# Second attention of a decoupled cross-attention kernel: four row tiles at once on packed copies of its values

## The chip, the cores and the metric

The kernel runs on one core of a Trainium2 chip. The metric is device microseconds from start to end of one execution; lower is better. Shortened below: PE is TensorE, DVE is VectorE, ACT is ScalarE, POOL is GpSimd, SP is SyncE (it issues most DMAs). PSUM is the memory that PE writes its products to, in banks of 512 fp32 values for each of 128 partitions; SBUF holds everything else on the core, HBM lies outside.

## What is computed

```python
# x (2, 2048, 640), ctx (2, 128, 384), 8 heads of 80, 4 tokens
enc, ca = ctx[:, :124], ctx[:, 124:]
hs = mha(x @ Wq, enc @ Wk, enc @ Wv)                  # text attention: 2048 queries, 124 keys
ca_q1 = einsum('btc,th->bch', ca, Wq_ca)              # 384 channels as queries
ca_q1 = ca_q1[:, np.linspace(0, 383, 2048).astype(int), :]
ca_hs1 = mha(ca_q1, x, x)                             # first attention, over 2048 rows of x
ca_hs2 = mha(ca_hs1 @ Wq, ca @ Wk_ca, ca @ Wv_ca)     # second attention, over 4 tokens
out = (hs + ca_hs2) @ Wout + b_out + x
```

All in fp32. Of the second attention only 384 rows per batch are distinct, since the queries repeat channels.

## The kernel before

The kernel computes the 384 distinct rows of the second attention for each of the two batches. Its values are multiplied with Wout beforehand (`values_weights`): a row for each pair of a head and a token, 640 columns wide, in `w2_sb`. The pairs lie in four groups, one for two heads each, that start at partitions 0, 32, 64 and 96; within a group stand 16 rows, for two batches, two heads and four tokens. So 112 rows are in use, the rows between groups are zero, and row 112 (`N2`) is `b_out`, loaded by a DMA of its own. What the second attention gives, times Wout and with the bias, is `o2`: 384 x 640 in HBM for each batch.

`second(b)` makes it. After the softmax over four tokens (`less`, an exponential on ACT, `share`), the weights lie in `p2`, 128 channels x 3 channel tiles x 8 heads x 4 tokens. `share` divides them and spreads them by two multiplications into `p2pad`, which POOL has cleared and whose column 112 it has set to one, in the places of batch b. `turn` transposes each 128 x 113 of it into a PSUM bank, ACT copies the three transposes to `p2T`, and for each of the three channel tiles and the two halves of 320 columns `by_columns` runs four matmuls of 113 x 32 against `w2_sb`, one for each 32 output partitions: four column strips, which PE runs side by side. Each product takes one of four single banks (`banks`), ACT copies it out, and when both halves of a channel tile are there, SP stores it.

An output row tile is 128 rows of x. For each, an indirect DMA on POOL (`add_second`, profile line L2324) gathers the rows of `o2` by the channel that each row uses and adds them to a buffer that was loaded with x; the tiles are called `x_more` and, for the later ones, `last_rows`. Then PE multiplies the text attention's heads (`hs`, `wout_sums`) with Wout into `po`, and DVE adds that to the buffer, which SP stores.

The first attention of a batch (`adapter`) runs in two passes over x, held in a compressed form `zop`. Pass one forms scores `s1` by four row tiles at once, each 32 rows deep and 512 columns wide, into four banks that form a single buffer, `quad` (tag `sq`); DVE takes the maximum (`mx`), and only then does the next round start. Pass two forms `s2` in the same buffer, ACT takes the exponential (`ea`), and PE contracts it with `y_sb` into `acc`. Beside this run the query projections (`pq`), the text scores (`sc`), their softmax (`m`, `p`, `r`), its transposition by DVE and DMAs (`eb`, `kept`, `pT`) and the text output (`ph`, `hs`, `po`). x comes in through `xi`, which DVE transposes to `xt`.

Every operation is a `Do(engine, function, after, needs, frees, marks, mode)`, yielded by a generator for each part of the work. `needs` names a room (a pool of buffers: `banks`, `quad`, `eas` for SBUF tiles), `frees` gives it back, `mode` is the tile shape of PE (rows, columns). The order is not found at build time: the table `TURNS` holds, for every operation, its place in one order of the whole program, so that each engine's instructions follow that order. Waits are then put in by the framework where an instruction uses what another engine or a DMA writes.

Most instructions are recorded by helpers, so a line of the profile tells the helper: L395 is `matmul`, L404 `by_columns`, L409 `transpose`, L426 any call of DVE, ACT or POOL, L446 `dma`. The trace cuts names at their numbers: it shows `po2` and `po` both as `po`, with `w_sb` for `w2_sb` among its inputs, `s1` and `s2` as `s`, `pt_p2` as `pt_p`, and `o2` as `o`.

Of the kernel before, what the change touches and what calls it, by code (L numbers as in the profile page):

```python
# [14 lines left out]
P = 128  # L15
# [50 lines left out]
class Desk:  # L66
# [19 lines left out]
        ".1": [731], ".2": [38, 53, 54, 72, 84, 96, 102, 114, 126, 144, 156, 168, 198, 216, 498, 702], ".3": [698],  # L86
        ".4": [5, 46, 64, 70, 82, 94, 112, 136, 244, 250, 262, 268, 274, 286], ".5": [414, 445, 504, 523, 594, 613,
        620], ".6": [11, 17, 138, 162, 192, 204, 330, 336, 348, 383], ".6.1": [122], ".6.2": [188], ".6.3": [302],
        ".6.4": [326], ".6.5": [152], ".6.6": [181], ".6.7": [211], ".6.8": [229], ".6.9": [343], ".6.10": [361],
        ".6.11": [368], ".7": [374, 456, 482, 824], ".8": [23, 29, 35, 174, 222, 234, 252, 276, 294, 306, 354, 426,  # L90
        474, 510, 546, 600, 636, 750, 1020, 1031], ".8.1": [320], ".8.2": [313], ".8.3": [572], ".8.4": [667],
        ".8.5": [1067, 1069, 1208, 1213, 1226], ".8.5.1": [1288], ".8.5.2": [1318], ".8.5.3": [1385], ".8.5.4":
        [1391, 1396, 1499, 1501, 1511, 1525], ".8.5.5": [1354], ".8.5.6": [1360], ".8.5.7": [1409], ".8.5.8": [1547,
        1582, 1715, 1753, 1901, 1993], ".9": [290, 389, 420, 462, 473, 540, 582, 593, 630, 648, 659, 678, 708, 720,
        774], ".9.1": [433], ".9.2": [535], ".9.3": [554], ".9.4": [608], ".9.5": [643], ".9.6": [674], ".9.7":
        [715], ".9.8": [734], ".9.9": [757], ".9.10": [794], ".10": [629, 660, 686, 764, 900, 920, 930, 991, 998,
        1008, 1046, 1050, 1076], ".11": [746, 786, 810, 828, 852, 912, 947, 953, 955, 968, 976, 1084, 1174, 1276,
        1378, 1453], ".11.1": [848], ".11.2": [836], ".11.3": [866], ".11.4": [908], ".11.5": [938], ".12": [1091,
        1095, 1280], ".13": [772, 784, 1186], ".14": [694, 1176, 1244, 1290, 1334, 1398, 1417, 1422, 1447], ".15":
        [580, 963, 984, 1056, 1248, 1260, 1343], ".15.1": [1016], ".15.2": [1118], ".15.3": [1268], ".15.4": [1303],  # L100
        ".16": [1467], ".17": [401, 1104, 1147, 1153, 1163, 1166, 1189, 1196, 1220, 1231, 1298], ".17.1": [1562,
        1576, 1604, 1654, 1745, 1751, 1942, 2638, 3298, 3574], ".18": [395, 1145], ".19": [1037, 2699], ".20": [406,
        412, 442, 454, 490, 496, 520, 532, 562, 569, 800, 806, 818, 842, 860], ".21": [875, 1788, 1825, 1831, 1841,
        1844, 1867, 1880, 1904, 1933, 2036], ".21.1": [1892, 1912, 1946, 2236, 2339, 2345, 2350, 2554, 2722, 4594],
        ".22": [887, 2147], ".23": [2123, 3653], ".24": [881, 1128, 1200, 1308, 1362, 1440, 1518, 1536, 1608, 1686,
        1716, 1818, 1884, 1914, 1986, 2106, 2117], ".24.1": [1429], ".24.2": [1555], ".24.3": [1873], ".24.4":
        [1951], ".24.5": [2159, 2161, 2216, 2225, 2227, 2300], ".24.5.1": [2248], ".24.5.2": [2254], ".24.5.3":
        [2375], ".24.5.4": [2381, 2386, 2501, 2605, 2705, 2803], ".24.5.5": [2308], ".24.5.6": [2398], ".24.5.7":
        [2513], ".24.5.8": [2837, 3022, 3185, 3271, 3281, 3361], ".25": [892, 898, 928, 982, 1102, 1114, 1126, 1138,
        1324, 1331, 1460, 1472, 1514, 1532, 1592], ".26": [1619, 2352, 2449, 2461, 2471, 2522, 2569, 2612, 2684,  # L110
        2749, 2792], ".26.1": [2504, 2566, 2624, 2776, 2957, 2963, 3016, 3316, 5062, 5350], ".27": [1631, 2927],
        ".28": [3065, 4643], ".29": [1625, 1637, 2081, 2442, 2490, 2544, 3059], ".29.1": [1851], ".29.2": [2133],
        ".29.3": [2169], ".29.4": [2187], ".29.5": [2849], ".29.6": [2921], ".29.7": [2070, 2208, 2280, 2532],
        ".29.7.1": [2754, 2874], ".29.7.1.1": [3038], ".29.7.2": [2136, 2256], ".29.7.2.1": [2293], ".29.7.3":
        [2574, 2706, 2808], ".29.7.3.1": [2660], ".29.7.3.2": [2858], ".29.7.4": [2179], ".29.7.5": [2263],
        ".29.7.6": [2366], ".29.7.7": [2557], ".29.8": [2591, 2593, 2642, 2651, 2653, 2678], ".29.8.1": [2998],
        ".29.8.2": [2668], ".29.8.3": [3101], ".29.8.4": [3389, 3400, 3551, 3637, 3659, 3661], ".29.8.5": [3250],
        ".29.8.6": [3376], ".29.8.7": [3515], ".29.8.8": [3707, 3826, 3947, 4213, 4223, 4315], ".30": [1642, 1666,
        1708, 1732, 1774, 1786, 1960, 1984, 2014, 2153, 2192, 2276, 2318, 2330, 2402], ".31": [2417, 3090, 3163,
        3169, 3179, 3206, 3289, 3434, 3464, 3517, 3632], ".31.1": [3554, 3748, 3902, 3928, 3995, 4001, 4072, 4630,  # L120
# [2444 lines left out]
```

## Time and profile before

| | us |
|---|---|
| median of 3 runs (lowest, highest) | 577.65 (577.57, 577.72) |
| profiled execution | 578.33 |
| its span, first to last instruction | 576.5 |
| PE busy | 566.8 (98%) |
| DVE busy | 395.6 (69%) |
| ACT busy | 297.4 (52%) |
| POOL busy | 151.3 (26%) |

The granted clock of PE was 1.00. 1.83 us of the profiled execution lie around the span. A page of the profile lists the instructions by line, engine, operation, output and inputs with their sum and mean; the trace behind it answers for one stretch, one engine or one tile. An engine's idle time is given with the engine or transfer that it waited for. PE's instructions come as weight loads (PEld) and matmuls; a matmul of fp32 operands leaves two records, one of the rounded type fp32r leaves one. Several matmuls in different strips or row tiles run side by side, so the sum of their durations says little; the start of the next group says how long they held PE.

### The profile page before, as it was taken

What the parts mean: (1) busy time and instruction counts of PE and PEld (TensorE: products, weight loads), DVE (VectorE), ACT (ScalarE), POOL (GpSimd) and SP (SyncE); (2) the same over time, 40 slices, a digit from 0 to 9 for tenths busy, and PEclk for the clock granted to TensorE, in tenths of its full rate; (3) what the DMA queues carried; (4) which work ended last, traced back from release to release, by engine and by line L of the source; (5) the groups of instructions that cost most, each with busy time, mean ns of one, the idle gap of its engine ahead of it and who ended that gap; (6) DMA issues with size and microseconds to landing.
All of it is one profiled execution on the core that took longest, in us unless ns stands there. A gap on an engine that the chain in (4) does not pass through costs nothing.

```text
span 576.5 us, 18994 instructions
## 1 busy us (share of the span) xinstructions
PE 566.8 (98%) x8115; PEld 311.3 (54%) x8115; DVE 395.6 (69%) x666; ACT 297.4 (52%) x840; POOL 151.3 (26%) x211
## 2 busy tenths in 40 slices
PE   9999999999999999999999999999999999999997
PEld 8885335455556455465554554554454454445463
DVE  2465899999998567468899999998243224435363
ACT  1222355565668698999957572634564763100000
POOL 8202023041520005301014151313332211345151
PEclk9999999999999999999999999999999999999999
DMA  7998475878748785535574988865676556879988
GB/s 221 225 247 128 145 152 154 180 181 177 208 117 177 219 231 137 177 111 182 181 238 145 321 273 241 239 231 157 164 208 192 147 155 213 222 191 260 280 164 226
DMA packets 145214, 112.70 MB, mean 195 GB/s; under 512 B 82405, under 2 KB 116581, under 8 KB 145130
## 3 DMA queue, kind: packets, MB, share of 16 engines
q1 hardware_dynamic: 139210, 100.47, 60.7%
q0 software_dynamic: 5632, 10.69, 11.0%
q8 instruction: 64, 1.05, 0.7%
q10 hardware_dynamic: 288, 0.33, 0.2%
q14 instruction: 20, 0.16, 0.1%
HBM read 71.23 MB, written 40.22 MB: 193 GB/s over the span
## 4 chain that ended last, share of the span: by engine, by line
PE 73%; DVE 13%; DMA 5%; ACT 4%; issue 3%; POOL 0%; SPq 0%; DVEq 0%; ACTq 0%
PE po L404 24%; PE pq L404 13%; PE acc L395 7%; PE ph L395 6%; PE s L395 6%; DVE mx L426 5%; PE sc L395 5%; PE pq L395 4%; PE pyz L395 2%; ACT ea L426 2%; ACT p L426 2%; DVE eb L426 2%; DMA x_more<-in_x_dram 1%; PE pv L395 1%; PE pk L395 1%
## 5 line engine op out<-in xcount | busy, mean ns | idle before, releaser
L426 DVE TENSOR_REDUCE mx<-s 128x4 f32<-128x2048 f32 x48 | 109.0, 2270 | 2.8 <-PE s L395 2.7
L426 ACT ACTIVATE p<-sc,m 128x124 f32<-128x124 f32 x256 | 90.2, 375 | 37.4 <-DVE m L426 37.4
L426 ACT ACTIVATE ea<-s 128x2048 f32<-128x2048 f32 x48 | 90.6, 1887 | 36.3 <-PE s L395 36.3
L404 PE MATMUL po<-wout_sums,hs 128*32 128x320 f32 x1024 | 78.6, 433 | 1.5 <-DVE x_more L426 1.5
L404 PE MATMUL po<-wout_sb,hs 128*32 128x320 f32 x928 | 72.0, 434 | 0.0
L404 PE MATMUL pq<-xt,wq_sb 128*32 128x256 f32 (+1 forms) x928 | 65.9, 418 | 0.0
L426 DVE TENSOR_TENSOR last_rows<-last_rows,po 128x320 f32<-128x320 f32 x60 | 28.2, 481 | 49.3 <-PE po L404 48.8
L426 DVE TENSOR_TENSOR x_more<-x_more,po 128x320 f32<-128x320 f32 x68 | 32.4, 481 | 42.4 <-PE po L404 40.7
L426 ACT ACTIVATION_READ_ACCUMULATOR p<-sc,m 128x1 f32 x256 | 55.4, 216 | 0.0
L404 PEld LDWEIGHTS po<-wout_sums,hs 128*32 128x32 f32 x1024 | 33.0, 110 | 34.4 <-DVE x_more L426 2.0
L426 POOL TENSOR_TENSOR p<-p,r 128x992 f32<-128x992 f32 x11 | 20.4, 1852 | 117.1 <-DVE r L426 117.1
L395 PE MATMUL acc<-ea,y_sb 128*32 128x384 f32 (+2 forms) x768 | 50.3, 383 | 0.2 <-ACT ea L426 0.2
L395 PE MATMUL ph<-pT,vpad 128*32 128x256 f32 x768 | 48.1, 381 | 0.1
L2324 POOL DMA_INDIRECT x_more<-o,query x17 | 26.7, 1568 | 80.6 <-DVE x_more L426 47.7
L426 DVE TENSOR_REDUCE m<-sc 128x4 f32<-128x496 f32 x64 | 40.8, 659 | 8.7 <-PE sc L395 8.6
L404 PEld LDWEIGHTS po<-wout_sb,hs 128*32 128x32 f32 x928 | 29.5, 110 | 30.1 <-issue 1.6
L404 PEld LDWEIGHTS pq<-xt,wq_sb 128*32 128x32 f32 x928 | 28.2, 110 | 28.3 <-issue 13.6
L426 DVE STREAM_TRANSPOSE eb<-p 128x1024 f32<-128x1024 f32 x32 | 39.4, 1232 | 2.7 <-ACT p L426 1.6
L395 PEld LDWEIGHTS sc<-kmain,q 64*128 64x128 f32 x512 | 31.2, 187 | 14.6 <-issue 7.4
L426 POOL TENSOR_TENSOR hs<-hs 128x256 f32<-128x256 f32 x32 | 25.7, 833 | 50.7 <-ACT hs L426 30.2
L395 PE MATMUL sc<-kmain,q 64*128 64x124 f32 x512 | 37.2, 284 | 0.0
L426 POOL TENSOR_TENSOR x_sums<-xt,x_sums 128x512 f32<-128x512 f32 x10 | 13.7, 1365 | 84.8 <-DVE x_sums L426 84.5
(219 smaller groups left out, 857.4 us busy)
## 6 DMA issues: line engine op xcount, KB each, us to landing
kept<-eb SPq DMA_DIRECT2D x32, 512.0 KB, 3.7
pT<-kept SPq DMA_DIRECT2D x16, 1024.0 KB, 8.1
landing<-away SPq DMA_DIRECT2D x15, 512.0 KB, 4.4
xi<-in_x_dram SPq DMA_DIRECT2D x56, 128.0 KB, 4.3
x_more<-in_x_dram SPq DMA_DIRECT2D x17, 320.0 KB, 5.2
out_dram<-x_more SPq DMA_DIRECT2D x16, 320.0 KB, 4.1
last_rows<-in_x_dram SPq DMA_DIRECT2D x15, 320.0 KB, 4.9
out_dram<-last_rows SPq DMA_DIRECT2D x14, 320.0 KB, 4.0
```

Source lines behind the costliest of these rows:

```text
L395: self.pin(self.nc.tensor.matmul(out, lhsT, rhs, **kw))
L404: self.pin(self.nc.tensor.matmul(out[j : j + 32], lhsT[:, j : j + 32], rhs, **kw))
L426: self.pin(getattr(engine, what)(*args, **kw))
L2324: desk.pin(nc.gpsimd.indirect_dma_start(out=t, out_offset=None, in_=o2_of[b], in_offset=bass.IndirectOffsetOnAxis(ap=query[:, st : st + 1] ...
```

## The change

The values are brought into a form in which 32 rows suffice for a batch: eight heads by four tokens, without the rows of the other batch and without zeros. `w2_sb` becomes 128 x 2 x 320. The products of `values_weights` are first put there as before, in 112 rows; half of `b_out`, broadcast to 16 rows by its DMA, is added to the first 16 rows, which are the first group, two heads, for both batches. Since each head's weights sum to one, the two halves make the whole bias. Four DMAs store the groups to HBM as `rows_w2`, 32 rows for each batch, and two for each batch bring them back: the left and the right half of the columns, 32 partitions each, twice.

`share` becomes one multiplication in place. `turn` turns the weights by matmuls with the identity in four column strips: it places the 32 rows of two channel tiles, each of them twice, in the four groups of partitions; a second set does so for the third channel tile. One copy brings both to `p2T`. The products then run in row tiles of 32 x 128 with 320 columns: a round of four, for two channel tiles and both halves, then one of two for the third tile. A round writes one bank of `quad` for each of its matmuls. Each channel tile is copied out by one copy of 640 columns, on ACT or on DVE, and stored. `quad` is given back after the copies of a round; the step that closes it after the last batch (`more`) now waits for it. The order of all work, the table `TURNS`, is another one; some instructions change engines with it (softmax scalings from ACT to POOL, sums of `hs` from DVE to POOL, copies).

```diff
@@ the table TURNS
-        ".1": [731], ".2": [38, 53, 54, 72, 84, 96, 102, 114, 126, 144, 156, 168, 198, 216, 498, 702], ".3": [698],
-        ".4": [5, 46, 64, 70, 82, 94, 112, 136, 244, 250, 262, 268, 274, 286], ".5": [414, 445, 504, 523, 594, 613,
...
+        ".1": [995], ".2": [38, 53, 54, 72, 84, 96, 102, 114, 138, 156, 162, 168, 204, 210, 804, 972], ".3": [590],
+        ".4": [5, 46, 64, 70, 82, 94, 112, 136, 244, 250, 262, 268, 274, 286], ".5": [420, 446, 468, 487, 534, 553,
...
@@
     krest = const.tile([P, 4, B, NK], F32R, name="krest")
     vpad = [const.tile([P, HEADS, VH + 2 * VR], F32, name=f"vpad_{b}") for b in range(B)]
     y_sb = const.tile([P, NSB, 4, 2, 4, G], F32, name="y_sb")
-    w2_sb = const.tile([N2 + 1, H], F32, name="w2_sb")
-    p2pad = const.tile([P, NCC, P], F32, name="p2pad")
+    w2_sb = const.tile([P, B, HALF], F32, name="w2_sb")
     query = const.tile([P, NST], mybir.dt.uint32, name="query")
     cap = ctx.enter_context(tc.tile_pool(name="cap", bufs=1))
     small = ctx.enter_context(tc.tile_pool(name="small", bufs=4))
@@
     for t in (caT, cadT, blk["k"], blk["v"]):
         nc.gpsimd.memset(t, 0.0)
     wqcaT = sp.tile([P, NCH, T], F32, name="wqcaT")
+    bias = sp.tile([2 * B * T, H], F32, name="bias")
@@
         def last():
             for h in range(HEADS):
                 dma(wout_sb[VR * h : VR * (h + 1), 4, :], Wout[D * h + VH : D * (h + 1), :], 0.1, 0.42, 1.6)
-            dma(w2_sb[N2:, :], b_out[None, :], 0.1)
+            dma(bias, b_out[None, :].to_broadcast([2 * B * T, H]), 0.1)
         yield Do("SP", last, marks=[("wout", 2)])
@@
                 "PE", product, ["blk v"] + [("wout", k) for k in range(3)], needs=[(banks, 1)]
             )
             yield evacuate(
-                w2_sb[:N2, cols], op.value[:N2], op.slots[0][0], after=[op.at], marks=[("w2", u)]
+                w2_sb[:N2, u, :], op.value[:N2], op.slots[0][0], after=[op.at], marks=[("w2 rows", u)]
+            )
+
+        def add_bias():
+            to = w2_sb[: 2 * B * T].rearrange("p u n -> p (u n)")
+            desk.v_scalar_tensor_tensor(to, bias, 0.5, to, ALU.mult, ALU.add)
+
+        yield Do("DVE", add_bias, [("w2 rows", 0), ("w2 rows", 1), ("wout", 2)], marks=["w2 made"])
+        rows_w2 = hbm.tile([B, G, H], F32, name="rows_w2")
+        for g in range(4):
+            yield Do(
+                "SP",
+                lambda g=g: dma(
+                    rows_w2[:, 2 * T * g : 2 * T * (g + 1), :],
+                    w2_sb[G * g : G * g + 2 * B * T].rearrange("p u n -> p (u n)"), 0.25, 0.42,
+                ),
+                ["w2 made"], marks=[("w2 out", g)],
+            )
+        for b in range(B):
+            halves_of_b = rows_w2[b].rearrange("k (u n) -> u k n", u=2)
+            yield Do(
+                "SP", lambda b=b, of=halves_of_b: [
+                    dma(w2_sb[2 * G * i : 2 * G * (i + 1), b, :], of, 0.45, 0.42) for i in range(2)
+                ],
+                [("w2 out", g) for g in range(4)], marks=[("w2", b)],
             )
     def text_values():
@@
                 desk.g_memset(e.rearrange("p h (j k) -> p h j k", j=4)[:, :, :, NK // 4 :], 0.0)
         yield Do(
-            "POOL", go, ["v done", "keys", "query", "wy 1", "wy 0", ("w2", 0), ("w2", 1), "wz"],
+            "POOL", go, ["v done", "keys", "query", "wy 1", "wy 0", "w2 made", "wz"],
             marks=["late"],
         )
@@
     def second(b):
-        def clear():
-            desk.g_memset(p2pad, 0.0)
-            desk.g_memset(p2pad[:, :, N2 : N2 + 1], 1.0)
-
-        op = yield Do("POOL", clear, [])
-        cleared = op.at
         N = NCC * HEADS
         s2 = s2f.rearrange("p a h t -> p (a h) t")
         p2 = small.tile([P, N, T], F32, tag="p2", name=f"p2_{b}", bufs=1)
@@
         def share():
             desk.v_tensor_reduce(r2, p2, AX.X, ALU.add)
             desk.v_reciprocal(r2, r2)
-            p2of = p2.rearrange("p (a g j) t -> p a g j t", a=NCC, j=2)
-            r2of = r2.rearrange("p (a g j x) -> p a g j x", a=NCC, j=2, x=1)
-            for j in range(2):
-                k0 = 2 * T * b + T * j
-                desk.v_tensor_tensor(
-                    p2pad[:, :, : 4 * G].rearrange("p a (g k) -> p a g k", g=4)[:, :, :, k0 : k0 + T],
-                    p2of[:, :, :, j, :], r2of[:, :, :, j, :].to_broadcast([P, NCC, 4, T]), ALU.mult,
-                )
-            desk.spent += 0.43
-
-        op = yield Do("DVE", share)
+            desk.v_tensor_tensor(p2, p2, r2.unsqueeze(2).to_broadcast([P, N, T]), ALU.mult)
+            desk.spent += 0.3
+
+        yield Do("DVE", share)
+        rounds = ((0, 1), (2,))
         def turn(s):
             pt = bank(s[0], f"pt_p2_{b}")
-            for ct in range(NCC):
-                transpose(pt[: N2 + 1, ct * P : (ct + 1) * P], p2pad[:, ct, : N2 + 1], ident)
+            for n, of in enumerate(rounds):
+                for g in range(4):
+                    ct = of[g // 2 % len(of)]
+                    matmul(
+                        pt[G * g : G * (g + 1), n * P : (n + 1) * P],
+                        p2[:, ct * HEADS : (ct + 1) * HEADS, :].rearrange("p h t -> p (h t)"), ident,
+                        start=True, stop=True, skip_group_check=True,
+                    )
             return pt
-        op = yield Do("PE", turn, [op.at, cleared], needs=[(banks, 1)])
+        op = yield Do("PE", turn, needs=[(banks, 1)], mode=(P, 32))
         pt, s = op.value, op.slots[0][0]
         def out_of(e):
-            t = ea_tile(e[0], f"p2T_{b}")[: N2 + 1, 0, :]
-            copy(t, pt[: N2 + 1, :CAD])
+            t = ea_tile(e[0], f"p2T_{b}", 512)[:, 0, : 2 * P]
+            copy(t, pt[:, : 2 * P])
             return t
         op = yield Do("ACT", out_of, needs=[(eas, 1)], frees=[(banks, s)])
         p2T, i = op.value, op.slots[0][0]
         here = op.at
         o2_of[b] = hbm.tile([CAD, H], F32, tag=f"o2_{b}", name=f"o2_{b}")
-        for ct in range(NCC):
-            op = yield Do("NONE", lambda e: ea_tile(e[0], f"o2_{b}_{ct}"), [here], needs=[(eas, 1)])
-            o2, k = op.value.rearrange("p g k -> p (g k)")[:, :H], op.slots[0][0]
-            for u in range(2):
-                cols = slice(u * HALF, (u + 1) * HALF)
-
-                def product(s, u=u, cols=cols):
-                    po = bank(s[0], f"po2_{b}_{ct}_{u}")
-                    by_columns(
-                        po[:, :HALF], p2T[:, ct * P : (ct + 1) * P], w2_sb[:, cols],
+        op = yield Do("NONE", lambda e: ea_tile(e[0], f"o2_{b}", 512), [here], needs=[(eas, 1)])
+        o2, k = op.value.rearrange("p g k -> p (g k)")[:, : NCC * H].rearrange("p (a n) -> p a n", a=NCC), op.slots[0][0]
+        for n, of in enumerate(rounds):
+
+            def product(s, n=n, of=of):
+                q4 = late["sq"].tile([P, 4, 512], F32, tag="sq", name=f"po2_{b}_{n}")
+                for g in range(2 * len(of)):
+                    part = slice(G * g, G * (g + 1))
+                    matmul(
+                        q4[:, g, :HALF], p2T[part, n * P : (n + 1) * P], w2_sb[part, b, :],
                         start=True, stop=True,
                     )
-                    return po
-
-                op = yield Do("PE", product, [here, ("w2", u)], needs=[(banks, 1)], mode=(P, 32))
-                op = yield Do(
-                    "ACT", lambda po=op.value, cols=cols: copy(o2[:, cols], po[:, :HALF]),
-                    frees=[(banks, op.slots[0][0])], marks=[("o2 part", b, ct, u)],
-                )
-            yield Do(
-                "SP", lambda: dma(o2_of[b][ct * P : (ct + 1) * P, :], o2, 1.2, 0.37),
-                [("o2 part", b, ct, 0), ("o2 part", b, ct, 1)], frees=[(eas, k)],
-                marks=[("o2 out", b, ct)],
-            )
-        yield Do(
-            "NONE", lambda: None, [("o2 out", b, ct) for ct in range(NCC)], frees=[(eas, i)],
-            marks=[("o2", b)],
-        )
+                return q4
+
+            op = yield Do("PE", product, [here, ("w2", b)], needs=[(quad, 1)], mode=(32, P))
+            for c, ct in enumerate(of):
+                yield Fork(one(Do(
+                    EITHER,
+                    lambda q4=op.value, c=c, ct=ct: copy(
+                        o2[:, ct].rearrange("p (u n) -> p u n", u=2), q4[:, 2 * c : 2 * c + 2, :HALF]
+                    ),
+                    [op.at], marks=[("o2 part", b, ct)],
+                )), 0)
+                yield Fork(one(Do(
+                    "SP", lambda ct=ct: dma(o2_of[b][ct * P : (ct + 1) * P, :], o2[:, ct], 1.2, 0.37),
+                    [("o2 part", b, ct)], marks=[("o2 out", b, ct)],
+                )), 0)
+            yield Do("NONE", lambda: None, [("o2 part", b, ct) for ct in of], frees=[(quad, 0)])
         if b == B - 1:
-            def more():
+            def more(at):
                 sq_stack.close()
                 late["ps"] = ctx.enter_context(tc.tile_pool(name="ps_r", bufs=1, space=bass.MemoryType.PSUM))
                 banks.at += [desk.now] * 4
-            yield Do("NONE", more, [])
+            yield Do("NONE", more, [], needs=[(quad, 1)])
+        yield Do(
+            "NONE", lambda: None, [("o2 out", b, ct) for ct in range(NCC)], frees=[(eas, i), (eas, k)],
+            marks=[("o2", b)],
+        )
     sq_stack = ExitStack()
     early_stack = ExitStack()
```

406 rows, old and new, of the table TURNS are left out of this document.

## Prediction

> **What bounds the kernel now.** I read the page's first part, then who holds TensorE up.
>
> ```profile
> PE 566.8 (98%) x8115; PEld 311.3 (54%) x8115; DVE 395.6 (69%) x666; ACT 297.4 (52%) x840; POOL 151.3 (26%) x211
> PE po L404 <- DVE x_more L426: 1.5, 2, 1.1
> PE s L395 <- ACT ea L426: 1.2, 2, 1.0
> PE s L395 <- DVE mx L426: 1.2, 2, 0.8
> ```
>
> TensorE (PE) is busy for 98% of the span, and its waits (total, times, longest) are tiny: 1.5 us for a finished output row, 2.4 us for the score buffer. So PE's own work is the first account, and a microsecond of it is a microsecond of time, unless another engine is nearly full as well. Whether one is, the table by stretch says, here its sums over the first attention of each batch, 65 to 178 us and 276 to 388 us:
>
> ```profile
> sum 113.00, PE 112.49 PEld 56.28 DVE 111.73 ACT 68.09 POOL 28.08; mean PE 18.75 PEld 9.38 DVE 18.62 ACT 11.35 POOL 4.68
> sum 112.00, PE 110.91 PEld 59.18 DVE 106.08 ACT 66.89 POOL 28.02; mean PE 22.18 PEld 11.84 DVE 21.22 ACT 13.38 POOL 5.60
> ```
>
> VectorE (DVE) is 99% busy in the first and 95% in the second, where 5.9 us are free. Both engines bind there together. Outside of these, PE alone binds (DVE is at 69% over the whole). Batch 0's second attention falls into the second stretch, batch 1's lies later, where DVE has room.
>
> **What is removed.** The order of PE for batch 0 (o2 is the second attention's output, `po2` its product, `pt_p2` the turning of its weights, `s1` the next scores), before and then after:
>
> ```order
> L409 MATMUL pt_p2_0_3959<-ident_69,p2pad_111 113x128 x3
> L404 MATMUL pq_7_0_3761<-xt_1_3_2898,wq_sb_98 32x256 x8
> L404 MATMUL pq_7_3_3978<-x_sums_841,wq_sb_98 32x256 x16
> L404 MATMUL po2_0_0_0_4000<-w2_sb_110,p2T_0_3974 32x320 x4
> L395 MATMUL s1_1_0_2_0_4008<-zop_1_0_3223,cop_153 128x512 x4
> L404 MATMUL po2_0_0_1_4018<-w2_sb_110,p2T_0_3974 32x320 x4
> ```
>
> ```order
> L395 MATMUL pt_p2_0_3942<-ident_69,p2_0_3697 32x128 x8
> L404 MATMUL pq_7_0_3750<-xt_1_3_2987,wq_sb_98 32x256 x8
> L395 MATMUL po2_0_0_3965<-w2_sb_110,p2T_0_3959 128x320 x4
> L404 MATMUL pq_7_3_3973<-x_sums_872,wq_sb_98 32x256 x16
> L395 MATMUL s1_1_0_2_0_3998<-zop_1_0_3211,cop_153 128x512 x4
> L404 MATMUL pq_7_4_4006<-xt_1_3_2987,wq4_99 32x512 x8
> ```
>
> A product of four column strips per channel tile and half becomes a round of four row tiles, for two channel tiles and both halves: two rounds a batch for six groups. The round takes the score buffer (`quad`), so it stands between two `s1` that need the same buffer. Their prices, from PE's timeline (start, length, tile, matmul records; an fp32 matmul leaves two records, a score matmul one):
>
> ```profile
> L404 PE MATMUL po<-w_sb,p2T 113*32 113x320 f32 x96 | 8.7, 435 | 0.1
> 346.72 0.72 PE L404 MATMUL po<-wout_sb,wout_sums 128*32 128x320 f32 x8
> 347.37 0.50 PE L395 MATMUL s<-zop,cop 32*128 32x512 f32 x4
> 347.81 2.90 PE L404 MATMUL po<-wout_sb,hs 128*32 128x320 f32 x40
> 350.64 0.51 PE L395 MATMUL s<-zop,cop 32*128 32x512 f32 x4
> 293.42 0.58 PE L409 MATMUL pt_p<-ident,p2pad 128*113 128x128 f32 x3
> 293.93 1.07 PE L404 MATMUL pq<-xt,wq_sb 128*32 128x256 f32 x16
> 294.82 1.91 PE L404 MATMUL pq<-x_sums,wq_sb 128*32 128x256 f32 x32
> ```
>
> Forty records (five groups of four) hold PE from 347.81 to 350.64, so 2.83; eight (one group) from 346.72 to 347.37, so 0.65. The difference of four groups is 2.18: 0.54 a group, with 0.11 for the change of shape to `s`. The 96 records are 12 groups: 6.5 us go. The old turning is 0.51 a batch (293.42 to 293.93): 1.0 goes. In all 7.5 us.
>
> **What is added on PE.** No row shows fp32 matmuls in four row tiles. The nearest are `s`, four row tiles of 512 columns in 0.44 (347.37 to 347.81), which is one pass, and fp32 in two row tiles, against fp32 alone:
>
> ```profile
> 288.76 1.16 PE L395 MATMUL sc<-kmain,q 64*128 64x124 f32 x16
> 289.68 0.64 PE L395 MATMUL sc<-krest,rests 64*128 64x124 f32 x8
> 44.90 1.78 PE L395 MATMUL pv<-w_v,ctxT 128*128 128x320 f32 x6
> 46.52 0.60 PE L409 MATMUL pt_a<-ident,a 128*128 128x128 f32 x4
> ```
>
> A whole fp32 matmul of 320 columns takes 0.54 (1.62 for three, 44.90 to 46.52), so 124 columns would take 0.21; eight of them in two row tiles took 0.92 (288.76 to 289.68) and not 1.67. So fp32 row tiles do run two at once, and four at once I take as 0.54 a round, the price of one: four rounds, 2.2. The bounds are this and 12 x 0.54 = 6.5, if all run one after the other. A round stands alone among strips, so it pays a change of shape, about 0.12: 0.5. The new turning is two groups of four strips of 128 columns a batch; strips of 256 columns took 0.89 for two groups (293.93 to 294.82), so 0.22 a group, 0.9 in all, with no change of shape around it. Added 3.5; **net on PE -4.0**.
>
> The Trainium skill (TensorE: Matmul & The Clock Gate, Measured speedup vs the span model) gives four row tiles of 512 columns as 3.07 times as fast, not 4 times. By that a round would be about 0.70 and the forecast 0.6 us later, an estimate from that page; this trace's four `s` in 0.44 speak for full overlap.
>
> **The copies out and the shared buffer.** Six copies of 320 columns a batch, all on ACT, become three of 640, on ACT or DVE.
>
> ```profile
> L426 DVE COPY hs<-ph 128x512 f32<-128x512 f32 x14 | 9.3, 683 | 7.1 <-PE ph L395 7.1
> L426 DVE COPY hs<-ph 128x256 f32<-128x256 f32 x3 | 1.2, 416 | 0.0
> L426 ACT COPY hs<-ph 128x512 f32<-128x512 f32 x18 | 10.5, 590 | 24.7 <-PE ph L395 24.6
> L426 ACT COPY o<-po 128x320 f32<-128x320 f32 x12 | 5.2, 430 | 15.1 <-PE po L404 15.1
> 508.00 0.04 issue
> 508.75 0.03 issue
> 508.77 0.02 DVEq L426
> 508.79 0.04 issue
> ```
>
> Carried on along each pair of rows, 640 columns are 0.82 on DVE and 0.70 on ACT. In the built order one engine's copy waits for the other's, so the buffer is held for both in sequence. A handover costs about 0.09 (0.03, 0.02 and 0.04 in the chain). After a round the next use of `quad` thus comes 0.82 + 0.70 + 3 x 0.09 = 1.8 us later. Batch 0's first round has 16 `pq` matmuls ahead of `s1`, 32 records, about 1.8: cover just fits, but two softmax reductions stand ahead of DVE's copy. The wait lies between 0 and 0.7; I take 0.35. Batch 1, before and then after (`po_9`, `po_12` are output rows, `ph_9` the text attention's values):
>
> ```order
> L395 MATMUL ph_9_0_6359<-pT_9_5766,vpad_1_108 32x256 x8
> L409 MATMUL pt_p2_1_6369<-ident_69,p2pad_111 113x128 x3
> L395 MATMUL ph_9_2_6375<-pT_9_5766,vpad_1_108 32x256 x8
> L404 MATMUL po2_1_0_0_6388<-w2_sb_110,p2T_1_6384 32x320 x4
> L395 MATMUL ph_9_4_6394<-pT_9_5766,vpad_1_108 32x256 x8
> L404 MATMUL po2_1_0_1_6406<-w2_sb_110,p2T_1_6384 32x320 x4
> ```
>
> ```order
> L395 MATMUL pt_p2_1_6353<-ident_69,p2_1_6237 32x128 x8
> L404 MATMUL po_9_2_6363<-wout_sb_100,hs_0_4125 32x320 x12
> L395 MATMUL po2_1_0_6383<-w2_sb_110,p2T_1_6377 128x320 x4
> L404 MATMUL po_9_0_6339<-wout_sums_4124,hs_0_4125 32x320 x8
> L395 MATMUL po2_1_1_6399<-w2_sb_110,p2T_1_6377 128x320 x2
> L404 MATMUL po_9_1_6403<-wout_sums_4124,hs_0_4125 32x320 x8
> ```
>
> Between its two rounds stand only two groups, 1.08: PE waits 1.8 - 1.1 = **0.7**, and between 0 and 1.5 with a busy ACT ahead. What is queued behind is PE's whole stream.
>
> **DVE.** In the second stretch PE now asks for the same scores in 2 us less, while DVE's work there stays the same (its instructions counted in both orders, each at its row's mean). The free 5.9 us shrink to 3.9; I charge 0.4 for tighter meetings, between 0 and 2.0 (all of batch 0's gain).
>
> **The late end.** The chain that ended last:
>
> ```profile
> 509.75 0.33 POOL x_more L2324
> 512.35 1.56 POOL last_rows L2324
> 514.22 6.45 DMA x_more<-o,query
> 520.68 5.37 DMA out_dram<-x_more
> 526.12 7.73 DMA x_more<-in_x_dram
> 533.94 0.50 DVE x_more L426
> 534.48 13.15 PE po L404 x192
> ```
>
> Batch 1's o2 reaches its first output rows at 514; they are stored, their buffer is loaded anew, and PE waits for that at 533, two waits and 1.5 us with the longest at 1.1. The new order finishes o2 some groups earlier (two rounds close together instead of six groups spread over PE's row), so the gathers start earlier. I count the longest wait as gone, **-1.1**, between -1.5 and 0.
>
> **Edits at nothing.** Scalings of the text probabilities on POOL:
>
> ```profile
> L426 POOL TENSOR_TENSOR p<-p,r 128x992 f32<-128x992 f32 x11 | 20.4, 1852 | 117.1 <-DVE r L426 117.1
> ```
>
> ACT's softmax scalings that move to GpSimd (POOL): six more at 1.85 are 11 us of the 425 that POOL has free, over the whole kernel; nothing I saw is waiting for one. The clearing of `p2pad` and one of two small multiplications: off the path. Half the bias, 16 rows of 640: one DVE instruction under 1 us in the 99% stretch, replaced by work moved out; uncovered, 1 us. The values' copies go out to HBM in four DMAs and back in four on SyncE (SP), and are needed 200 us later; only what is queued behind them matters (below).
>
> **The sum.** -4.0 + 0.35 + 0.7 + 0.4 - 1.1 = -3.65 (unrounded -3.6). The profiled execution is 578.33 us: 576.5 of span and 1.83 around it. It becomes 574.7, and the median of the runs, 0.68 below it, 574.0.
>
> **The rivals.** *PE alone counts:* no added wait and both late waits gone, -4.0 - 1.5, 572.2. For it: PE's waits are tiny now.
>
> *DVE binds the second stretch:* batch 0's 2.0 us and its 0.35 come to nothing, 0.4 is still paid; -2.0 + 0.7 + 0.4 - 1.1 = -2.0, 575.7. For it: 95% of DVE; against: 5.9 us free. The Trainium skill (TensorEngine Tiling (Array Packing), PSUM Bottleneck) warns that after a fourfold speedup of TensorE the copy out of PSUM may become the bottleneck; here that is the 1.8 us held after a 0.54 round. If the bias and a later second half of the values also delay the first stretch by 1.5, 577.2: no change.
>
> *Row tiles don't overlap:* 4.3 more on PE, 578.3: no change. Against: the `sc` rows.
>
> *SP becomes late, the other side:* SP's order near 90 to 105 us, before and then after (`xi` are loads of x that DVE transposes, `rows_w2` and `w2_sb` the values' copies out and back):
>
> ```order
> L446 DMA xi_0_3_885<-in_x_dram 32x16x32
> L446 DMA kept_1_1139<-eb_1_0_1129 512x1x256
> L446 DMA y_0_1_963<-yt_0_1_1_1017 512x1x128
> L446 DMA away_1_1107<-x_sums_841 32x4x256 x2
> L446 DMA away_1_1107<-wq_sums_821 32x4x256
> L446 DMA y_sb_109<-y_0_1_963 32x4x256
> L446 DMA landing_823<-away_1_1107 128x1x1024
> L446 DMA away_1_1107<-wq_sums_821 32x4x256
> L446 DMA xi_1_0_1238<-in_x_dram 32x32x32
> ```
>
> ```order
> L446 DMA xi_0_3_800<-in_x_dram 32x16x32
> L446 DMA rows_w2_816<-w2_sb_110 2x8x640
> L446 DMA y_sb_109<-y_0_0_669 32x4x256
> L446 DMA y_0_1_971<-yt_0_1_1_1023 512x1x128
> L446 DMA kept_1_1150<-eb_1_0_1140 512x1x256
> L446 DMA away_1_1092<-x_sums_872 32x4x256
> L446 DMA away_1_1092<-wq_sums_835 32x4x256
> L446 DMA away_1_1092<-x_sums_872 32x4x256
> L446 DMA w2_sb_110<-rows_w2_816 64x1x320 x2
> L446 DMA away_1_1092<-wq_sums_835 32x4x256
> L446 DMA w2_sb_110<-rows_w2_816 64x1x320 x2
> ```
>
> Where loads and stores of the first attention followed each other, copies stand between, and those coming back wait for those going out.
>
> ```profile
> 65.14 0.58 SPq L446 DMA_DIRECT2D first_rests<-away  x1
> 70.44 0.54 SPq L446 DMA_DIRECT2D y<-yt  x1
> o<-o SPq DMA_DIRECT2D x6, 320.0 KB, 3.0
> L426 DVE STREAM_TRANSPOSE xt<-xi 128x512 f32<-128x512 f32 x35 | 22.7, 679 | 1.6 <-DMA xi<-in_x_dram 1.6
> ```
>
> Eight issues at 0.54 are 4.3 us, and a wait for a landing 3.0: 7.3. DVE has no free time there, and has waited for `xi` already. If all of it reached DVE, -3.6 + 7.3, 581.4; slower from 4.8 us on. Against: `xi` was late in one wait of 1.6 us over the kernel, and SP issued nothing there from 65.7 to 70.4, 4.7 us that can take most of the new ones.
>
> **How the numbers follow.** Forecast 0.55 (572.6 to 575.2), PE alone 0.09, DVE binds the second stretch 0.16, both stretches 0.06, no overlap 0.04, SP late 0.10. The likeliest is 574.0. The range takes the first three, 0.80: 572.0 to 576.6. What this measurement can tell from no change is 0.2%, 1.2 us: faster below 576.5, 0.80; the two cases near 577 to 578, 0.10; slower 0.10.
>
> **What would show it.** Four `po2` rounds of about 0.55 each on PE; a wait of PE near 0.7 ahead of batch 1's second round, on DVE's copy; no wait near 533; DVE's sums in the two stretches still 111 to 112 and about 106, in 113 and 110 us. I am wrong if a round takes over 1 us, if batch 1's output still meets its rows late, or if DVE shows idle time on `xi` between 65 and 178 us.

## The result, and the profile after

The changed kernel takes 580.99 us (median of 20 runs, 579.60 to 586.82) against 577.90 for the kernel before (20 runs): 1.0062 times its time, 95% interval 1.0040 to 1.0083. Forecast was 574.0, within 572.0 to 576.6. The profiled execution took 581.29, with a span of 579.4 against 576.5. The ratios here and below leave out three runs of the experiments that came out slow (583.82 of `wide_back`, 586.64 of `late_back` and 944.77 of `before_wide`), which the medians and the counts of runs include.

Who holds TensorE up now (the page's first part, and the waits of PE: total, times, longest):

```profile
PE 565.4 (98%) x8069; PEld 308.1 (53%) x8069; DVE 398.2 (69%) x659; ACT 282.0 (49%) x793; POOL 166.0 (29%) x219
PE sc L395 <- ACT p L426: 2.2, 2, 1.4
PE ph L395 <- DMA pT<-kept: 1.6, 1, 1.6
PE s L395 <- ACT ea L426: 1.4, 3, 1.0
PE po L404 <- DVE hs L426: 1.3, 2, 0.8
PE unread L395 <- DVE zeros L426: 1.1, 1, 1.1
PE pt_x L409 <- DMA xz<-in_x_dram: 0.8, 1, 0.8
PE s L395 <- DVE mx L426: 0.8, 2, 0.4
PE po L395 <- DVE o L426: 0.5, 1, 0.5
```

The wait for `x_more` (1.5 us) is nearly gone, as forecast, and the one ahead of batch 1's second round (`po <- DVE o`, 0.5) is there. New and not forecast are the first two rows and the fourth. The largest loss lies where DVE is full. The stretch 105 to 125 us, first of the kernel before, then of the changed one (busy times of PE, PEld, DVE, ACT, POOL; clock; DMA share; GB/s):

```profile
105.00:125.00 20.00, 19.95 (x328) 11.39 (x316) 19.91 (x27) 11.12 (x46) 6.89 (x5) 1.00 0.83 181
```

```profile
105.00:125.00 20.00, 17.81 (x256) 9.65 (x248) 16.96 (x23) 10.88 (x43) 5.34 (x4) 0.91 0.76 154
```

PE stands still for 2.2 us of it, DVE for 3.0, and PE's clock falls to 0.91 in the mean. What led there is read from the changed kernel's SP issues (start, length), then ACT's timeline (first of the kernel before, where no wait stands ahead of the cast, then of the changed one), then the chain that ended last:

```profile
100.29 1.16 SPq L446 DMA_DIRECT2D w_sb<-rows_w  x2
101.55 0.56 SPq L446 DMA_DIRECT2D away<-wq_sums  x1
102.17 1.15 SPq L446 DMA_DIRECT2D w_sb<-rows_w  x2
103.83 0.56 SPq L446 DMA_DIRECT2D y<-yt  x1
104.49 1.01 SPq L446 DMA_DIRECT2D landing<-away  x1
```

```profile
108.51 0.63 ACT L426 CAST rests<-landing 128x512 fp32r<-128x512 f32 x1
```

```profile
114.02 0.62 ACT L426 CAST rests<-landing 128x512 fp32r<-128x512 f32 x1 [4.60 <-DMA landing<-away]
```

```profile
104.49 9.51 DMA landing<-away
...
115.15 2.08 ACT p L426 x12
...
118.50 1.55 PE sc L395 x22
```

`landing` is a load of 512 KB on which the text scores' second term waits; its fifteen loads in the kernel before took 3.8 to 5.6 us, this one 4.8. Here one is issued right behind the four copies back of the values and takes 9.51. ACT stands 4.6 us for it, with the text softmax (`p`) queued behind; PE's next scores (`sc`) wait for that softmax's buffer, and DVE's next maximum stands behind the softmax's reciprocal. Then PE runs at half clock:

```profile
115.00:118.00 3.00, 1.30 (x14) 0.48 (x6) 0.94 (x2) 3.00 (x17) 1.53 (x1) 1.00 0.66 195
118.00:122.00 4.00, 3.50 (x42) 2.21 (x42) 3.02 (x4) 3.41 (x15) 0.00 (x0) 0.76 0.98 168
122.00:126.00 4.00, 4.00 (x60) 1.98 (x64) 4.00 (x4) 1.89 (x11) 0.00 (x0) 0.81 1.15 153
```

4 us at 0.76 and 4 at 0.81 are 1.7 us lost, one piece of 3.41 us at half clock. So this place costs 2.2 + 1.7 = 3.9 us, as much as the change takes off PE's work:

```profile
296.97 0.64 PE L395 MATMUL pt_p<-ident,p 128*32 128x128 f32 x16
297.43 1.05 PE L404 MATMUL pq<-xt,wq_sb 128*32 128x256 f32 x16
298.46 0.82 PE L395 MATMUL po<-w_sb,p2T 32*128 32x320 f32 x8
299.21 1.93 PE L404 MATMUL pq<-x_sums,wq_sb 128*32 128x256 f32 x32
...
500.69 0.81 PE L395 MATMUL po<-w_sb,p2T 32*128 32x320 f32 x4 [0.51 <-DVE o L426]
501.43 1.00 PE L404 MATMUL po<-wout_sums,hs 128*32 128x320 f32 x10
```

A turning holds PE 0.46 (296.97 to 297.43), a round 0.75 (298.46 to 299.21) or 0.74, changes of shape included. Two turnings and four rounds are 3.9 us; in the kernel before the same slots were 7.8.

### The profile page after: what moved, and what is told of

It is laid out like the page before. It is cut to its first block, busy times and chain, and to the rows that moved or that the text cites. A ratio compares the mean times of both kernels' runs of the same rounds, so it can differ in the third digit from the quotient of the medians.

```text
span 579.4 us, 18870 instructions
## 1 busy us (share of the span) xinstructions
PE 565.4 (98%) x8069; PEld 308.1 (53%) x8069; DVE 398.2 (69%) x659; ACT 282.0 (49%) x793; POOL 166.0 (29%) x219
## 4 chain that ended last, share of the span: by engine, by line
PE 78%; DVE 9%; DMA 6%; ACT 3%; SPq 2%; issue 2%; DVEq 0%; ACTq 0%
PE po L404 26%; PE pq L404 17%; PE acc L395 7%; PE sc L395 6%; PE ph L395 6%; PE s L395 6%; PE pq L395 4%; DVE mx L426 3%; DMA landing<-away 3%; PE pyz L395 2%; DMA pT<-kept 1%; SPq L446 1%; ACT ea L426 1%; PE pk L395 1%; DMA xz<-in_x_dram 1%
## 5 line engine op out<-in xcount | busy, mean ns | idle before, releaser
L404 PE MATMUL po<-wout_sb,hs 128*32 128x320 f32 x1024 | 79.1, 434 | 0.9 <-DVE hs L426 0.8
L426 POOL TENSOR_TENSOR p<-p,r 128x992 f32<-128x992 f32 x17 | 32.4, 1906 | 146.5 <-DVE r L426 146.5
L404 PE MATMUL pq<-xt,wq_sb 128*32 128x256 f32 (+1 forms) x928 | 67.2, 424 | 0.0
L426 POOL TENSOR_TENSOR hs<-hs 128x256 f32<-128x256 f32 x37 | 34.7, 992 | 58.5 <-DVE hs L426 40.1
L404 PEld LDWEIGHTS po<-wout_sb,hs 128*32 128x32 f32 x1024 | 32.6, 110 | 33.3 <-issue 1.7
L395 PE MATMUL ph<-pT,vpad 128*32 128x256 f32 x768 | 46.6, 380 | 1.6 <-DMA pT<-kept 1.6
L2346 POOL DMA_INDIRECT last_rows<-o,query x15 | 23.3, 1551 | 55.0 <-DVE last_rows L426 41.5
```

Of the source, the lines that this page charges most:

```text
L395: self.pin(self.nc.tensor.matmul(out, lhsT, rhs, **kw))
L404: self.pin(self.nc.tensor.matmul(out[j : j + 32], lhsT[:, j : j + 32], rhs, **kw))
L426: self.pin(getattr(engine, what)(*args, **kw))
L2346: desk.pin(nc.gpsimd.indirect_dma_start(out=t, out_offset=None, in_=o2_of[b], in_offset=bass.IndirectOffsetOnAxis(ap=query[:, st : st + 1] ...
```

## The experiments

My theory after the traces: the four copies back are cut so that few of the DMA engines carry them. Counted in the trace's packet records, their 256 packets of 1280 bytes lie between 101.6 and 110.8 us at 55 ns each (median), which is 14 us of packet time in 9.2: one or two engines of sixteen at a time. If so, a load that is spread over all engines waits behind them on those. The rivals: eight more DMAs on SP make `landing` late, however they are cut; or the new order puts ACT's cast where it would wait anyway.

**The copies cut in another way** (`wide_back`), and **moved away** (`late_back`):

```diff
-            halves_of_b = rows_w2[b].rearrange("k (u n) -> u k n", u=2)
...
-                    dma(w2_sb[2 * G * i : 2 * G * (i + 1), b, :], of, 0.45, 0.42) for i in range(2)
...
+                    dma(
+                        w2_sb[G * q : G * (q + 1), :, :],
+                        rows_w2[:, :, HALF * (q % 2) : HALF * (q % 2 + 1)].rearrange("b k n -> k b n"), 0.45, 0.42,
+                    )
+                    for q in (2 * b, 2 * b + 1)
```

> The changed kernel, its four copies back from HBM cut in another way: each brings 32 partitions of both batches (rows of 1280 bytes, 64 of them, outermost dimension 32) instead of 64 partitions of one batch (outermost dimension 2). Same bytes, number, place in SP's order. Theory (few DMA engines: the copies as written run 128 packets one after another on two of the 16 DMA engines, and the load 'landing' behind them takes 9.5 us instead of 4.4, ACT stands 4.6 us, PE 2.2 us, and the clock then halves for 3.4 us): landing within 5.5 us, ACT's wait for it under 1 us near 110, no clock drop, 3 to 4 us less than the changed kernel: 577.2, about the kernel before. Rival (number: eight more DMAs on SP issue landing 3.4 us late): nothing changes, 581. Rival (order: in the new order ACT's cast stands ahead of the softmax and would wait anyway): 581.

Measured: 576.86 (13 runs), 0.9985 times the kernel before (0.9968 to 1.0003), where the changed kernel has 1.0062: 4.1 us less by the medians. DVE and PE are full again from 105 to 125 us:

```profile
sum 20.00, PE 20.00 PEld 11.42 DVE 20.00 ACT 12.78 POOL 5.33; mean PE 20.00 PEld 11.42 DVE 20.00 ACT 12.78 POOL 5.33
```

Both rivals had said 581. The order of all work and the number of DMAs are those of the changed kernel. `landing` is issued at 103.56 us here, and ACT hardly waits for it:

```profile
108.92 0.62 ACT L426 CAST rests<-landing 128x512 fp32r<-128x512 f32 x1 [0.28 <-DMA landing<-away]
```

So it took 5.3 us, within the 5.5 that were forecast. The same 256 packets of the copies lie within 2.8 us now (100.7 to 103.5 us, by the packet records). The execution that was profiled is the longest of the 13, 583.82; its pieces at half clock lie near 431 to 437 and 557 us, none of them here.

`late_back` keeps the narrow cut and changes two numbers of the order's table:

```diff
-        1636, 1648, 1834, 2020, 2398, 2440], ".15": [682, ...
+        1636, 1648, 1834, 2020, 5482, 5488], ".15": [682, ...
```

> The changed kernel with the same four narrow copies back, moved in SP's order by about 110 us, into the second pass of the first attention (near 215 us), where DVE is not full. Few DMA engines: landing takes 4 to 5 us and is issued 2 us earlier, no wait of ACT near 110, 577.2; a transfer near 215 us takes longer, at no cost. Number of DMAs: the four stores stay, the four loads go, so about half is won: 579. Order: 581.

Measured: 579.80 (12 runs), 1.0013 (0.9991 to 1.0036), less was won than the 577.2 of my theory; by its time alone this can't be told from "about half is won". The trace tells them apart: `landing` takes 5.2 us (issued at 104.05, ACT's cast at 109.27 behind a wait of 0.27), so the loss near 110 us is gone. It has come up at another place. The narrow copies are issued at 207.4 us there, and the next store behind them, `kept` (512 KB, median 3.7 us in the kernel before), takes twice its time; the chain of this kernel runs through it to the softmax, for which PE waits 1.1 us at 221, a wait that no other kernel here has there:

```profile
210.90 7.88 DMA kept<-eb
```

Half of its runs have a piece at half clock (a mean clock of 0.997 or less). Moving narrow copies moves their cost.

**The same loads in the kernel before**, ahead of the same `landing`, cut narrow (shown) and wide (`x[b, : 2 * G, :n]` as the source):

```diff
+    filler = const.tile([P, 256], F32, name="filler")
...
+        def land():
+            if m == 2:
+                for b, (to, n) in enumerate(((p2pad.rearrange("p a k -> p (a k)"), 320), (filler, 256))):
+                    for i in range(2):
+                        dma(to[2 * G * i : 2 * G * (i + 1), :n], x[b, :G, : 2 * n].rearrange("k (u n) -> u k n", u=2), 0.45, 0.42)
+            dma(t.rearrange("p g n -> p (g n)"), by_rows, 2.0, 0.56)
```

> The kernel before with four loads of x added right ahead of that landing, as the copies back are cut: 64 partitions each, outermost dimension 2, rows of 1280 bytes twice and of 1024 bytes twice (there is no room for more); nothing reads them. Few DMA engines: landing takes 8 to 10 us; it has 3 us of room in this order, so ACT's cast comes 4 us late, the softmax 1.5 to 2 us, and the time rises by 1.5 to 3.5 us: 579.2 to 581. Number: landing is issued 2.4 us later, within its room, and takes 4.4: 577.7, at most 578.2. Order: 577.7.

> The same four extra loads ahead of landing in the kernel before, with the same bytes, rows and partitions, but read from 64 rows of x, so that the outermost dimension is 64. Few DMA engines: landing takes 4 to 5.5 us, the time is the kernel before's within 0.6: 577.7 to 578.3. Number: the same as with the narrow loads.

Measured: narrow 582.87 (6 runs), 1.0087 (1.0067 to 1.0107), wide 578.95, 1.0017 (1.0002 to 1.0032). By the ratios, four small loads cost 5.0 us or 1.0 us, by their cut alone. Both times lie above what I had expected (579.2 to 581, and 577.7 to 578.3). The landings in the first attention of batch 0 (shortest, median, longest), narrow and then wide, and the stretch 105 to 125 us of the narrow one:

```profile
DMA to landing us min/median/max: 4.5/5.1/9.0
```

```profile
DMA to landing us min/median/max: 3.9/4.7/6.0
```

```profile
sum 20.00, PE 17.60 PEld 10.78 DVE 16.28 ACT 9.05 POOL 6.88; mean PE 17.60 PEld 10.78 DVE 16.28 ACT 9.05 POOL 6.88
```

The narrow kernel has the changed kernel's loss in the old order: a landing of 9.0 us, PE still for 1.97 us at 115 us, then 3.41 us at half clock. Of the 5.0 us, 1.7 are the clock's, which I had left out. The number of DMAs counts as well, by about a fifth of it. The Trainium skill (DMA: Bandwidth & Descriptors, Rules for kernel authors) says that an outermost dimension of size c below 16 confines a DMA to at most c engines; for c = 2 these traces agree, with one or two engines at a time in the changed kernel and 9.0 us against 6.0 here. Which engines carried a packet is not shown by the profile, so the count rests on the packet times.

**The clock.** Is it PE's own idle time that halves it?

```diff
-                        for g in range(4):
+                        for g in 5 * (0, 1, 2, 3) if (b, sb, ct, u) == (0, 2, 0, 0) else range(4):
```

(`hold_more` has 8 for 5.)

> The changed kernel, with one score round (batch 0, third block of x, first channel tile) computed five times over, on PE alone: 1.8 us more of PE's work right where it stands still near 116 us waiting for the softmax. The copies and the late landing stay. Theory: PE's clock halves for 3.4 us after PE stood still for 2.2 us out of 2.7; with under 1 us left of that the clock stays at 1.00 and 1.7 us are won though PE does more: 579.3. Rival (the halving has another cause, or the stall is DVE's and ACT's alone): 581, or up to 582.5 with PE's extra work.

> The changed kernel with the same score round computed eight times over (3.1 us more of PE's work), so that PE has hardly any idle time near 116 us; the copies, the late landing and ACT's wait stay. With five times the clock had still halved, after a gap of 1.4 us that lay in one stretch of 3.41 us between two possible changes of the clock. Theory (PE's idle share in one such stretch halves the clock in the next): no stretch at half clock near 120 us; 1.7 us are won there and up to 0.5 lost to the extra work, so about 579.3 and the stretch 118 to 122 at a clock of 1.00. Rival (the halving belongs to the stall of the whole chain, not to PE's idle time): a clock of 0.5 for 3.4 us as before.

With five times (579.57, 10 runs; 1.0041, 1.0016 to 1.0066) the clock still halved in the profiled execution: the second wait stayed whole. So the time that I had named came out, but not for the reason that I gave. With eight times the wait is 0.56 and the clock stays. PE's timeline and the stretch after it, first of `hold_clock`, then of `hold_more`:

```profile
118.27 0.94 PE L395 MATMUL sc<-kmain,q 64*128 64x124 f32 x12 [1.41 <-ACT p L426]
```

```profile
118.00:122.00 4.00, 3.73 (x42) 2.35 (x42) 3.08 (x4) 3.41 (x15) 0.00 (x0) 0.70 1.07 173
```

```profile
118.12 0.94 PE L395 MATMUL sc<-kmain,q 64*128 64x124 f32 x12 [0.56 <-ACT p L426]
```

```profile
118.00:122.00 4.00, 3.88 (x62) 2.64 (x66) 3.90 (x5) 3.41 (x14) 0.00 (x0) 1.00 1.04 176
```

ACT's wait was the same (4.7 and 4.5 us), so the idle time of PE decides. The mean clocks of all runs agree, though they don't say where a halved piece lies: one below 0.998 is in 16 of the changed kernel's 20 runs, in 5 of 10 with five times and in 2 of 12 with eight times. The time of this second kernel, 580.33 (12 runs; 1.0034, 1.0012 to 1.0056), missed the 579.3 that I had named: its extra scores delay DVE, and in its profile PE waits 1.0 us for DVE near 131 us instead.

**What a round costs** (each round computed nine times, on top of `wide_back`):

```diff
-                for g in range(2 * len(of)):
+                for g in [g for _ in range(9) for g in range(2 * len(of))]:
```

> The kernel wide_back with each of the four row-tile rounds computed nine times over, to read what a round costs on PE without the changes of tile shape around it: full overlap 0.54 each, and 32 more are 17 us; as the Trainium skill's 3.07 for four tiles would have it about 0.70, 22 us; one after the other 2.2 for a round of four. A round of two matmuls costs the same 0.54 with full overlap.

```profile
293.41 5.13 PE L395 MATMUL po<-w_sb,p2T 32*128 32x320 f32 x72
298.47 0.42 PE L404 MATMUL pq<-x_sums,wq_sb 128*32 128x256 f32 x4
```

Measured: 593.58 (one run), 16.7 us above `wide_back`'s median. Nine rounds hold PE 5.06, one held it 0.75: 4.31 for eight, 0.54 each; a round of two gives the same (5.04). So four fp32 row tiles overlap fully. The Trainium skill (TensorE: Matmul & The Clock Gate, Measured speedup vs the span model) gives 3.07 for four row tiles, by which a round would be about 0.70, an estimate; these rounds don't bear it out. The change of shape around a round is 0.75 - 0.54 = 0.21.

**The wait that the new order brings.** In the changed kernel PE waits 1.6 us near 433 us for `pT`, a load of 1 MB (in the profile of `wide_back` 2.9, of `late_back` 1.2). The chain of the changed kernel shows the load issued when the text output before it had given its buffer back, and 8.66 us on the way:

```profile
425.48 0.86 PE ph L395 x16
426.34 0.06 PE po L404
426.40 8.66 DMA pT<-kept
435.06 0.04 issue
435.11 1.05 PE ph L395 x13
```

Between lie 7.1 us of PE's work. The table of the order was edited so that 2.4 us more lie between, in `wide_ph` with the three products next to each other, in `wide_ph2` apart:

```diff
-        ".71.3": [10817, 10871, 10876, 11010, 11034, 11124, 11135], ".71.3.1": [11053], ".71.3.2": [11102],
+        ".71.3": [10817, 10871, 10876, 11118, 11130, 11148, 11159], ".71.3.1": [11119], ".71.3.2": [11132],
```

```diff
-        ".71.3": [10817, 10871, 10876, 11010, 11034, 11124, 11135], ".71.3.1": [11053], ".71.3.2": [11102],
+        ".71.3": [10817, 10871, 10876, 11082, 11118, 11166, 11177], ".71.3.1": [11089], ".71.3.2": [11120],
```

> The kernel wide_back with three products of one text output (unit 15, ph) moved on PE behind two output rows, two contractions and a score round, 2.4 us of work: in the new order PE reaches ph 1.2 to 2.9 us before its 1 MB load pT has landed (8.7 us after its buffer came free); the kernel before had no such wait. If that wait is a loss of its own, from the new order and not from the copies, it goes: 1.2 to 2.5 us less than wide_back, 575; with it goes a halved clock in some runs. If it only moves to the next use of the load, or the moved work then waits itself: 576.9 as wide_back.

> The kernel wide_back with the three products of unit 15's text output moved back by 2.4 us of PE's work as in wide_ph, but kept apart by contractions and score rounds, so that their copies out keep up. In wide_ph the wait for the load pT went and two waits for those copies came, 1.6 us. If that was all, PE has no wait over 0.5 us near 430 and the kernel gains 1.2 to 2.5 on wide_back: 575 to 575.7, below both kernels. If the wait moves once more: 576.9.

`wide_ph`: 577.27 (12 runs), 0.9992 (0.9973 to 1.0011), nothing won; the wait for the load went, two others came, since three products in a row outrun their copies (the lines have other numbers, as the table is laid out on more of them; `ph` is `matmul` still):

```profile
PE ph L806 <- DVE hs L837: 0.9, 1, 0.9
PE ph L806 <- ACT hs L837: 0.7, 1, 0.7
```

`wide_ph2`: **575.71 (12 runs), 0.9971 (0.9948 to 0.9994)**, faster than the kernel before and the changed one. Against `wide_back` (0.9968 to 1.0003) the intervals overlap, so these runs don't settle what the wait was worth. The execution profiled is the shortest of the 12, 574.37: its span was 572.3, PE was busy for 563.1 us of it (566.8 in the kernel before), and near 436 us one wait of 0.4 is left:

```profile
PE ph L408 <- DVE hs L439: 0.4, 1, 0.4
```

**The copies wide and late** (`wide_late`, the edits of `wide_back` and `late_back` together):

> The kernel wide_back with its four copies back moved to near 215 us. Few DMA engines: little is left to win, as the landing in wide_back still takes 5.9 us and ACT waits 1 us: 576.5, between 575.9 and 576.9. If the mere number of loads ahead of landing counts (the 1 us that four spread loads cost the kernel before), 576.

Measured: 577.44 (12 runs), 0.9986 (0.9967 to 1.0005), no better than `wide_back` and above the range that I gave. The 5.9 us in my expectation were misread: they are those of the first `landing`, at 72.55 us. The one behind the copies takes 5.3 in `wide_back` and 5.4 here, so there was nothing to win.


## Why the prediction was wrong

- *PE's work*: forecast -4.0, measured -3.9 from the slots (7.8 to 3.9). That the two agree so well is partly luck: 7.8 went where I had 7.5, and 3.9 came where I had 3.5. A round's matmuls were right at 0.54, the change of shape was not: 0.21 a round, not 0.12.
- *The step that failed* is in "Edits at nothing": the values' copies. Of the rival on SP I saw the place (the copies stand among the first attention's transfers), its sign and nearly its time (581.4), but gave it 0.10 and a wrong mechanism: I counted issues and one wait, and looked at `xi` and DVE; the free stretch of SP that I set against it, 65.7 to 70.4, lies 30 us ahead of the copies back (100.3 to 103.3). That its time came so near is luck. I read the 64 partitions of a copy and not its outermost dimension. The cost came from how the copies are cut, in the time of one landing (9.5 for 4.8 us), through ACT's queue, and nearly half of it from the clock, which I did not consider. At nothing in the sum, they cost 3.9 us in the trace and 4.1 by the medians of the changed kernel and `wide_back`. `wide_back` and the pair in the kernel before show it. The copies are not all: `wide_back`, without their cost, still lies 2.9 above the 574.0.
- *The new order* was read for where the changed products stand, and I took PE's small waits for a property that would stay. It brought waits of its own: 1.6 us for `pT` and 0.8 for `hs` near 494, which recur in the profiles of the other kernels of this order (the first in all but `wide_ph` and `wide_ph2`). `wide_ph2` shows that the first can be taken away, but not clearly what it is worth; of the second I only have the traces. The 0.5 for `hs` near 535 and the 0.8 for `xz` at the start are in no other profile of this order and belong to that one execution. Two others, of 583.82 (`wide_back`) and 585.00 (`hold_more`), have 2.3 and 2.0 near 555 us, where `hs` on POOL stands behind a gather that waits for a load of x, and the clock halves behind them: part of what spreads the runs.
- *The late end*: forecast -1.1, and the wait of 1.06 us for `x_more` near 533 went; in the changed kernel's profile 0.55 for `hs` came at the same place.
- *The shared buffer*: 0.5 measured for 0.7 ahead of batch 1's second round; nothing ahead of batch 0's scores (the gaps near 314 us are 0.79 before, 0.76 after), where I had 0.35.
- *DVE in the second stretch* did not swallow batch 0's gain: over the 24 maxima of batch 1's first attention, from 279 to 388 us, the changed kernel wins 1.2 us on the kernel before (from 3.56 late to 2.34 late), of 2.1 less work in the slots. My terms for it give 1.25 (2.0 less 0.35 and 0.4), though not by these two waits; where the rest went I can't say.

Summed for the two profiled executions: -3.9 of work; +2.2 and +1.7 at 116 us; +1.6 `pT`; +1.3 `hs`; +0.5 the round; +0.8 at the start; -1.3 for `x_more`; -0.2 for the scores: +2.7, of 2.9 measured. In the profile of `wide_ph2` the gain that was forecast seems to be there, 572.3 for a span of 572.9 foreseen, but that is its shortest run. Its median moved less, 2.0 us against the kernel before's in the same comparison, about half of the 3.65 forecast. Where the other half stays is open; a single execution of either kernel varies by more than that.

## What to carry to other kernels

Small copies that are off the path still take DMA engines: before you cost a transfer at nothing, look at its outermost dimension and at which load stands behind it, and what that load's reader has queued behind it. In a kernel where TensorE is 98% busy, a wait of 1.4 to 2.3 us cost 1.7 us more here where it halved the clock. A new order of all work is a change of its own: each load and each shared buffer has to be followed through it, not only the instructions that were meant.

## What was not expected of the hardware

- Four loads of 80 KB or less, cut with an outermost dimension of 2, lengthen a 512 KB load behind them from 4.8 to 9.0 and 9.5 us; cut with 32 or 64, it takes 5.3 and 6.0. Without them (`late_back`) it takes 5.2 in the new order.
- The clock changed only at multiples of 3.413 us from its first rise in every trace here, and how PE's idle time falls into these stretches seems to decide what follows. Of the stretches at full clock, those with 1.41, 1.42, 1.95, 1.97, 2.01, 2.04 and 2.31 us idle were followed by one at 0.5; none below 1.4 us was, nor were two with 1.43 (at the end of PE's work, in `before_wide`) and 1.59 (in `wide_ph`), so idle time alone draws no sharp line. A gap of 2.13 us that such a boundary cut into 1.3 and 0.8 left the clock alone, in the profile of `rounds_nine`. Where the boundaries fall differs from run to run (the first rise lies 4.0 to 7.0 us into the span in the 12 traces): of the changed kernel's 20 runs 16 show a mean clock below 0.998, of the kernel before's 79 beside the experiments 10. The Trainium skill (TensorE: Matmul & The Clock Gate, What's actually happening) tells of a free-running window of 3413 ns, which these traces bear out. The Trainium skill (TensorE: Matmul & The Clock Gate, HAM oscillation) gives as the rule no idle gaps of PE over about 3.4 us; here 1.41 us in one stretch were enough.
